# Row 1's bias and half of two rows' lo parts move between engines, and the first loads go through one queue

## The chip, the cores and the metric

The kernel runs on one core of one Trainium2 chip. A core has TensorE (matrix products; PE in the profile, PEld for its weight loads), VectorE (DVE), ScalarE (ACT), GpSimd (POOL) and SyncE (SP), which here only issues DMA transfers. SBUF is the on-chip memory with 128 partitions; PSUM holds the results of TensorE in eight banks of 128 x 512 float32. GpSimd reads and writes SBUF only in this kernel. The metric is device microseconds (us) from start to end of an execution, the median of some runs; lower is better.

## The reference

```python
# x: (4, 1024, 512), cond: (4, 256), W: (1536, 512), b: (512,)
hidden = concatenate([cond, cond], axis=-1)            # (4, 512)
x_mean = mean(x, axis=1, keepdims=True)                # (4, 1, 512)
fused = concatenate([x, x_mean * ones, hidden * ones], axis=-1)   # (4, 1024, 1536)
relation = relu(einsum('bld,do->blo', fused, W) + b)
out = x + relation
```

W falls into three parts of 512 rows. Only the first meets every row of x. The other two give one vector of 512 for each of the four batch rows r: mean(x) times the second part, plus cond times the sum of the two halves of the third part, plus b. That vector is the row's bias. So out = x + relu(x W_x + bias_r). All is float32.

## The kernel before, in words

**Tiles.** A row r has 8 tiles of 128 positions, so there are 32 tiles t = 0 to 31. A product needs x with its features on the partitions, so x must be turned. Four pieces j of 128 features each make up the sum, and each piece is multiplied in three matmuls, because a float32 value is split into hi (as rounded to the chip's fp32r type) and lo (the rest): hi by W's hi, hi by W's lo, lo by W's hi (L458 to L462). One tile takes 12 matmuls into one of five PSUM banks (pool ps_o).

**Turning.** Tiles are grouped in units: row 0 has units of 1, 1, 2 and 4 tiles, the other rows two units of 4. For row 0 TensorE turns the tiles of x against an identity matrix (L252). For rows 1 to 3 x is loaded a second time in 32-position blocks, as tile z, and VectorE turns those (L254). Either way the turned piece xT lies in PSUM, in a pool of two banks. ScalarE writes hi from it, and in the same instruction adds up the piece along the positions for the mean (L265); VectorE subtracts to get lo (L281). There are 15 buffers each of hi and lo. W's first part is split in the same way (w_hi on ScalarE, L233; w_lo on VectorE or GpSimd, L235).

**Bias.** VectorE adds up the sums of a row (total, L336) and forms acc = sum over j of total_j times W_mean_j plus the row's cond term (mean_term, L341, four instructions). The cond terms come from GpSimd and ScalarE (L332, L348, L353). acc is split into hi and lo (L357, L361), and two matmuls with a matrix of 1/1024 sum it over the partitions and spread it (bias_product, L373). What happens then depends on the row. Rows 0 and 1 (r < BY_PE = 2): the bias is split into a tile of 64 partitions, 32 with hi and 32 with lo (L384, L388), and a matmul with a 64 x 128 matrix "even" adds it into the tile's bank (L470); ScalarE applies relu straight from the bank (L480). Rows 2 and 3: ScalarE copies the bias to SBUF (L379), VectorE adds it to the bank's content into SBUF, which frees the bank (L477), and ScalarE applies relu there. The first three tiles (t < KEEP = 3) are finished before any bias is there: ScalarE copies their products to SBUF (L473), and VectorE adds the bias later (L477). GpSimd adds x (L485), SyncE stores (L497). There are ten output buffers. The last tile is done in two halves, with the bias product inside its bank, and VectorE does relu and the addition of x (L490).

**Order.** A planner in the file (class Plan) writes the order out beforehand. Each piece of work has a cost in us, an engine or two that may do it, what it depends on and an urgency; the planner keeps a clock for each engine, takes the work that could start first, and among work for that engine that could start within 0.1 us the most urgent. Every engine then works through its own instructions strictly in that order, as its inputs arrive. Loads and stores go through SyncE in such an order too.

**The first loads.** SyncE issues x of tile 0, of tile 1, of tiles 2 and 3, of tiles 4 to 7, then W's third part (w_cond) and W's second (w_mean), then the z loads of row 1 and on. Beside it ScalarE issues W's first part in four loads of 256 KB (L202). Eleven matmuls on zeros (L144) run ahead of all of it. The four loads of W have a buffer of their own; x tiles, in groups of four, share a pool of four buffers with w_cond.

The planner's line that makes a VectorE subtraction out of a piece, and the one that ties a turn to a free bank, are these:

```python
plan.add(("lo", c), {"dve": 0.15 + 0.135 * w}, [("hi", c)], urgent - 0.1, lambda e, c=c: split_lo(c))
if c >= 2:
    deps.append(("lo", c - 2))
```

Of the kernel before, what the change touches and what calls it, by code (L numbers as in the profile page):

```python
# [68 lines left out]
def kernel(  # L69
# [22 lines left out]
    nc = tc.nc  # L92
# [15 lines left out]
    Z_AHEAD, X_AHEAD, T_AHEAD = 24, 8, 7  # L108
    TURN_PE = (0, 1, 2, 3)
    BY_PE = 2  # L110
    KEEP = 3

# [53 lines left out]
    piece_of = {(u, j): c for c, (u, js) in enumerate(pieces) for j in js}  # L166
    first_piece = [min(c for (u, _), c in piece_of.items() if units[u][0] == r) for r in range(B)]
# [3 lines left out]
    w_x = const.tile([P, J, D], F32, name="w_x")  # L171
# [33 lines left out]
    plan.done["x", 1] = (9.8, 2.0, "sp")  # L205
# [4 lines left out]
    plan.done["cond"] = (12.7, 2.0, "sp")  # L210
    nc.sync.dma_start(out=w_mean, in_=Wv[1])
    plan.done["w_mean"] = (15.3, 2.0, "sp")
    plan.free["sp"] = 15.3
# [5 lines left out]
    x_order = [0, 1, None] + list(range(2, B * NK // G))  # L219
    for n, g in list(enumerate(x_order))[3:]:  # L220
        was = x_order[n - X_BUFS] if n >= X_BUFS else -1
        deps = ([] if was == -1 else [("add_cond", k) for k in range(KH)] if was is None else
                [("finished", was * G + i) for i in range(G)])
# [20 lines left out]
    def turn(c):  # L244
        u, js = pieces[c]
        n = units[u][2]
        v = xT[c] = ps_x.tile([P, G * P], F32, tag="x", name=f"xT{c}")
        if u in TURN_PE:
            for i in range(n):
                x_t = x_tile(last_tile[u] - n + 1 + i).rearrange("p (a j) -> p j a", j=J)  # L250
                for m, j in enumerate(js):
                    nc.tensor.transpose(v[:, (m * n + i) * P : (m * n + i + 1) * P], x_t[:, j], ident)  # L252
        else:
            nc.vector.transpose(  # L254
                v[:, : n * P].rearrange("p (n t) -> p n t", t=Q),
                zs[u].rearrange("p n (a j) -> p n j a", j=J)[:, : n * NQ, js[0], :],
            )

# [19 lines left out]
    def split_lo(c):  # L278
        u, js = pieces[c]
        m = units[u][2] * len(js) * P  # L280
        nc.vector.tensor_tensor(  # L281
            lo[c][:, :m], xT[c][:, :m], hi[c][:, :m].bitcast(F32), ALU.subtract
        )

    for c, (u, js) in enumerate(pieces):
        r, k0, n = units[u]

        urgent = 2 * c - 99.5 if not r else r * NK - T_AHEAD + (c - first_piece[r]) * 0.75
        deps = ([x_here(t) for t in range(last_tile[u] - n + 1, last_tile[u] + 1)]
                if u in TURN_PE else [("z", u, i) for i in range(NQ)])  # L290
        if c:
            deps.append(("turn", c - 1))
        if c >= 2:
            deps.append(("lo", c - 2))
            if len(pieces[c - 2][1]) > 1:
                deps.append(("sum", c - 2))
# [13 lines left out]
        if len(js) > 1:  # L310
            plan.add(("sum", c), {"dve": 0.65}, [("turn", c)], urgent + 0.1, lambda e, c=c: add_up(c))
# [52 lines left out]
    even32 = const.tile([2 * Q, P], F32, name="even32")  # L364
    nc.gpsimd.memset(even32, 1.0 / Q)
    even = const.tile([2 * Q, P], F32R, name="even")
    nc.gpsimd.tensor_copy(even, even32)

    def bias_product(r):
        m = 2 * Q if 0 < r < BY_PE else P  # L370
        pbs[r] = ps_b.tile([P, 512], F32, tag="b", name=f"pb{r}")
        for n, v in enumerate((acc_hi[r], acc_lo[r])):
            nc.tensor.matmul(  # L373
                pbs[r][:m], lhsT=mean[:, :m], rhs=v, start=(n == 0), stop=(n == 1)
            )
# [5 lines left out]
    def bias_hi(r):  # L381

        rows[r] = small.tile([2 * Q, D], F32R, tag="row", name=f"row{r}")
        nc.scalar.activation(rows[r], pbs[r][: 2 * Q], AF.Copy)  # L384

    def bias_lo(r):
        q = slice(Q, 2 * Q)
# [9 lines left out]
    for r in range(B):  # L397
        urgent = r * NK - 1.5 - 6 * (r == 0)
# [3 lines left out]
        for n in range(KH + J):  # L402
# [11 lines left out]
            else:  # L414
                deps = [("total", r), "w_mean"]
                if r and n == KH:
                    deps += [("bias", r - 1)] + [("bias_copy", 0)] * (r == 1)
# [8 lines left out]
        if r < BY_PE:  # L426
            plan.add(("bias_hi", r), {"act": 0.61}, [("bias_product", r)], urgent - 0.5,
                     lambda e, r=r: bias_hi(r))
            plan.add(("bias", r), {"dve": 0.69}, [("bias_hi", r)], urgent - 0.5,
                     lambda e, r=r: bias_lo(r))  # L430
            if not r:
                plan.add(("bias_copy", r), {"act": 0.61}, [("bias_product", r)], urgent - 0.4,
                         lambda e, r=r: bias_copy(r))
        else:
            plan.add(("bias", r), {"act": 0.61}, [("bias_product", r)], urgent - 0.5,
                     lambda e, r=r: bias_copy(r))
# [5 lines left out]
    def product(t, j, h=None):  # L442
# [15 lines left out]
        for n, (v, m) in enumerate(((hi, w_hi), (hi, w_lo), (lo, w_hi))):  # L458
            nc.tensor.matmul(  # L459
                pos[key][:, :w], lhsT=v[p][:, c], rhs=m[:, j, d],  # L460
                start=(h is None and j == 0 and n == 0), stop=((t < KEEP or r >= BY_PE) and j == J - 1 and n == 2),
            )  # L462
# [12 lines left out]
    def add_bias(t):  # L475
        o = o_tile(t)
        nc.vector.tensor_tensor(o, o if t < KEEP else pos[t], biases[t // NK], ALU.add)  # L477

# [20 lines left out]
    for t in range(NT):  # L499
        r, k = divmod(t, NK)  # L500
        u = unit_of[r, k]
        for h in (0, 1) if t == LAST else (None,):
            for j in range(J):
                c = piece_of[u, j]
                deps = [("hi", c), ("lo", c), ("w_hi", j), ("w_lo", j)]
                if j:
                    deps.append(("product", t, j - 1) if not h else ("product", (t, h), j - 1))
                elif h:
                    deps.append(("product", t, J - 1))
                else:  # L510
                    if t > 1:
                        deps.append(("product", t - 1, J - 1))
                    if t >= O_BANKS:
                        deps.append(("freed", t - O_BANKS))
                    if h == 0:
                        deps.append(("acc_lo", r))
                        deps.append(("freed", t + 1 - O_BANKS))
                plan.add(("product", (t, h) if h else t, j), {"pe": 0.7 if h is None else 0.36},
                         deps, t + 0.2 * j if t > 1 else 0.2 * j, lambda e, t=t, j=j, h=h: product(t, j, h))
        if t == LAST:  # L520
            for h in (0, 1):
                deps = [("product", (t, h) if h else t, J - 1), x_here(t)]
                if not h:
                    deps.append(("stored", t - O_BUFS))
# [4 lines left out]
        deps = [("product", t, J - 1), ("bias", r)]  # L529
        room = [("stored", t - O_BUFS)] if t >= O_BUFS else []  # L530
        if t < KEEP:
            plan.add(("freed", t), {"act": 0.6}, deps[:1], t, lambda e, t=t: keep(t))
            plan.add(("added", t), {"dve": 0.75}, [("freed", t), ("bias_copy", r)], t + 8, lambda e, t=t: add_bias(t))
            plan.add(("relu", t), {"act": 0.63}, [("added", t)], t + 8, lambda e, t=t: relu(t))
            biased = ("relu", t)
        elif r < BY_PE:
            plan.add(("biased", t), {"pe": 0.24}, deps, t, lambda e, t=t: bias_to_bank(t))
            plan.add(("freed", t), {"act": 0.63}, [("biased", t)] + room, t + 2, lambda e, t=t: relu(t))
            biased = ("freed", t)
        else:  # L540
            plan.add(("freed", t), {"dve": 0.7}, deps + room, t + 2, lambda e, t=t: add_bias(t))
# [3 lines left out]
            else:  # L545
                biased = ("freed", t)
# [37 lines left out]
```

## Time and profile before

| | us |
|---|---|
| median of 3 runs (117.93 to 118.69) | 118.6 |
| the profiled execution | 117.44 |
| its span, first to last instruction | 115.7 |
| TensorE busy | 107.7 |
| VectorE busy | 81.0 |
| GpSimd busy | 57.8 |
| ScalarE busy | 53.4 |

The profile comes from one execution. Its span is 1.7 us shorter than its time, since the time has a start and an end that the span leaves out. Busy times are sums over the whole span, and matmuls overlap one another, so that TensorE is called busy also where its matmuls follow slowly. The share of each stage has to be read from the stretches of the span. In a group of instructions, the number behind the x is how often it comes; behind the bar stand its busy time in all, the mean of one in ns, and the idle time of the engine ahead of it.

### The profile page before, as it was taken

The numbers are of one execution on the slowest core, as the hardware profiler recorded it, in microseconds if no ns is written. First come the engines' busy times: TensorE is split into PE (matmuls) and PEld (weight loads), VectorE is DVE, ScalarE is ACT, GpSimd is POOL, SyncE is SP. The second block draws the span as 40 slices with busy tenths as digits, with TensorE's granted clock in tenths as the row PEclk, the third lists the DMA queues.
The fourth block names the chain that finished last, engine by engine and source line by source line (L and its number), as shares of the span: only waits on it lengthen the run. The fifth ranks groups of instructions, "written<-read, shape, count | busy, mean of one in ns | idle before, by whom it ended". The sixth has DMA issues, their size and how long they took to land.

```text
span 115.7 us, 1477 instructions
## 1 busy us (share of the span) xinstructions
PE 107.7 (93%) x466; PEld 82.9 (72%) x466; DVE 81.0 (70%) x114; ACT 53.4 (46%) x122; POOL 57.8 (50%) x55
## 2 busy tenths in 40 slices
PE   5926999999999999999999999999999999999980
PEld 2415788888766687877766688887888878888870
DVE  1066734399999999976896999939999980632250
ACT  5055547887568460424963542246466140642200
POOL 6507144899809643040893029508354913199400
PEclk9998599999999999999999999999999999999999
DMA  3799999999999959999959999994422422025351
GB/s 109 179 392 396 394 370 198 203 203 205 205 256 281 199 136 207 304 388 390 349 177 213 272 397 407 400 258 176 164 91 106 169 91 91 0 91 222 140 227 45
DMA packets 22999, 26.31 MB, mean 227 GB/s; under 512 B 1228, under 2 KB 13776, under 8 KB 22864
## 3 DMA queue, kind: packets, MB, share of 16 engines
q1 hardware_dynamic: 22352, 25.17, 75.7%
q10 hardware_dynamic: 576, 1.05, 3.1%
q8 instruction: 3, 0.05, 0.2%
q14 instruction: 4, 0.03, 0.1%
q0 software_dynamic: 64, 0.01, 0.0%
HBM read 17.83 MB, written 8.39 MB: 227 GB/s over the span
## 4 chain that ended last, share of the span: by engine, by line
PE 89%; DMA 7%; SPq 1%; DVE 0%; issue 0%
PE po_None L459 77%; DMA x<-in_x_dram 7%; PE po_None L470 4%; PE xT L252 3%; PE po L459 2%; PE pb L373 2%; SPq L178 1%; PE po L455 0%; DVE o L490 0%; PE pt L324 0%
## 5 line engine op out<-in xcount | busy, mean ns | idle before, releaser
L485 POOL TENSOR_TENSOR o<-o,x 128x512 f32<-128x512 f32 x30 | 38.7, 1315 | 38.9 <-ACT o L480 32.1
L459 PE MATMUL po_None<-w_hi,hi 128*128 128x512 f32 x124 | 50.8, 409 | 0.0
L459 PE MATMUL po_None<-w_lo,hi 128*128 128x512 f32 x124 | 49.4, 398 | 0.0
L459 PE MATMUL po_None<-w_hi,lo 128*128 128x512 f32 x124 | 49.3, 398 | 0.0
L459 PEld LDWEIGHTS po_None<-w_hi,hi 128*128 128x128 f32 x124 | 23.5, 190 | 7.1 <-issue 1.6
L459 PEld LDWEIGHTS po_None<-w_hi,lo 128*128 128x128 f32 x124 | 23.6, 190 | 5.7
L459 PEld LDWEIGHTS po_None<-w_lo,hi 128*128 128x128 f32 x124 | 23.6, 190 | 5.0
L281 DVE TENSOR_TENSOR lo<-xT,hi 128x512 fp32r<-128x512 f32 (+1 forms) x34 | 21.9, 647 | 7.2 <-ACT hi L265 7.2
L254 DVE STREAM_TRANSPOSE xT<-z 128x512 f32<-128x512 f32 x24 | 26.2, 1102 | 0.3
L265 ACT ACTIVATE hi<-xT 128x512 fp32r<-128x512 f32 (+1 forms) x34 | 19.3, 571 | 9.3 <-DVE xT L254 5.5
L477 DVE TENSOR_TENSOR o<-po_None,bias 128x512 f32<-128x512 f32 x15 | 9.8, 677 | 12.2 <-ACT bias L379 4.1
L480 ACT ACTIVATE o<-o 128x512 f32<-128x512 f32 x17 | 10.5, 631 | 7.5 <-DVE o L477 7.5
L480 ACT ACTIVATE o<-po_None 128x512 f32<-128x512 f32 x13 | 7.5, 601 | 7.9 <-PE po_None L470 7.9
L341 DVE SCALAR_TENSOR_TENSOR acc<-w_mean,tot,acc 128x512 f32<-128x512 f32 x12 | 9.1, 756 | 0.4
L252 PE MATMUL xT<-ident,x 128*128 128x128 f32 x32 | 6.0, 307 | 3.5 <-DMA x<-in_x_dram 3.5
L252 PEld LDWEIGHTS xT<-ident,x 128*128 128x128 f32 x32 | 5.1, 207 | 4.6 <-issue 2.5
L357 ACT ACTIVATE acc_hi<-acc 128x512 fp32r<-128x512 f32 x4 | 2.4, 600 | 11.9 <-DVE acc L341 11.9
L265 ACT ACTIVATION_READ_ACCUMULATOR hi<-xT 128x1 f32 x32 | 6.4, 201 | 0.0
L353 POOL TENSOR_TENSOR cond<-bL,term 128x512 f32<-128x512 f32 x4 | 5.2, 1303 | 2.0 <-ACT term L348 2.0
L341 DVE SCALAR_TENSOR_TENSOR acc<-w_mean,tot,cond 128x512 f32<-128x512 f32 x4 | 5.7, 1426 | 0.6 <-POOL cond L353 0.3
L348 ACT ACTIVATE term<-wc,cT 128x512 f32<-128x512 f32 x8 | 5.6, 723 | 0.7 <-POOL cond L353 0.7
L353 POOL TENSOR_TENSOR cond<-cond,term 128x512 f32<-128x512 f32 x4 | 5.5, 1383 | 0.3
(54 smaller groups left out, 60.7 us busy)
## 6 DMA issues: line engine op xcount, KB each, us to landing
out_dram<-o SPq DMA_DIRECT2D x31, 256.0 KB, 2.4
x<-in_x_dram SPq DMA_DIRECT2D x7, 1024.0 KB, 7.9
z<-in_x_dram SPq DMA_DIRECT2D x24, 256.0 KB, 7.4
w_x<-in_L_cond_W_dram ACTq DMA_DIRECT2D x4, 256.0 KB, 7.2
w_cond<-in_L_cond_W_dram SPq DMA_DIRECT2D x1, 1024.0 KB, 12.7
w_mean<-in_L_cond_W_dram SPq DMA_DIRECT2D x1, 1024.0 KB, 12.6
x<-in_x_dram SPq DMA_DIRECT2D x2, 256.0 KB, 4.1
x<-in_x_dram SPq DMA_DIRECT2D x1, 512.0 KB, 8.0
```

The costliest lines, as they stand in the source:

```text
L252: nc.tensor.transpose(v[:, (m * n + i) * P : (m * n + i + 1) * P], x_t[:, j], ident)
L254: nc.vector.transpose(v[:, : n * P].rearrange("p (n t) -> p n t", t=Q), zs[u].rearrange("p n (a j) -> p n j a", j=J)[:, : n * NQ, js[0], :],)
L265: nc.scalar.activation(hi[c][:, :m], xT[c][:, :m], AF.Copy, accum_out=sums[:, r, js[0], s : s + 1] if len(js) == 1 else None,)
L281: nc.vector.tensor_tensor(lo[c][:, :m], xT[c][:, :m], hi[c][:, :m].bitcast(F32), ALU.subtract)
L341: nc.vector.scalar_tensor_tensor(acc[r], w_mean[:, j, :], totals[r][:, j : j + 1], acc[r] if j else conds[r], ALU.mult, ALU.add,)
L348: nc.scalar.activation(terms[r, k], wc[:, k], AF.Copy, scale=cT[:, k, r : r + 1])
L353: nc.gpsimd.tensor_tensor(conds[r], conds[r] if k else bL, terms[r, k], ALU.add)
L459: nc.tensor.matmul(pos[key][:, :w], lhsT=v[p][:, c], rhs=m[:, j, d], start=(h is None and j == 0 and n == 0), stop=((t < KEEP or r >= BY_P ...
L470: nc.tensor.matmul(pos[t], lhsT=even, rhs=rows[t // NK], start=False, stop=True)
L477: nc.vector.tensor_tensor(o, o if t < KEEP else pos[t], biases[t // NK], ALU.add)
L480: nc.scalar.activation(o_tile(t), pos[t] if KEEP <= t < BY_PE * NK else outs[t], AF.Relu)
L485: nc.gpsimd.tensor_tensor(outs[t], outs[t], x_tile(t), ALU.add)
```

## The change

- For rows 1 and 2, the pieces j = 1 and 3 of both units (8 of the 16) are turned by VectorE into SBUF, in a pool of two buffers, and their lo is made by GpSimd. The other pieces keep PSUM and VectorE. A turn waits for the lo of the piece two back of its own kind.
- BY_PE goes from 2 to 1: row 1's bias is copied to SBUF and added by VectorE, as in rows 2 and 3. Row 0 keeps the matmul, now with 128 rows (64 of hi, 64 of lo).
- The bias add of tiles 0 to 2 moves from VectorE to GpSimd.
- The first loads are all issued by SyncE in this order: x of tile 0, W's first 256 KB, x of tile 1, the other three of W, x of tiles 2 and 3, of 4 to 7, w_cond, w_mean.
- W's first part takes a buffer in the pool of x tiles; tiles 8 to 11 of x later get that buffer.
- Four more matmuls on zeros are put behind the turn of tile 0. Some urgencies change (T_AHEAD 7 to 8; the bias work of a row from 1.5 to 4 tiles ahead of it).

```diff
-    Z_AHEAD, X_AHEAD, T_AHEAD = 24, 8, 7
+    Z_AHEAD, X_AHEAD, T_AHEAD = 24, 8, 8
-    BY_PE = 2
+    BY_PE = 1
+    LO_POOL = {(r, u, j) for r in (1, 2) for u in (0, 1) for j in (1, 3)}
+    N_FILL = 4
+    by_pool = {c for c, (u, js) in enumerate(pieces)
+               if (units[u][0], units_of_row[units[u][0]].index(u), js[0]) in LO_POOL}
-    w_x = const.tile([P, J, D], F32, name="w_x")
+    w_x = xpool.tile([P, J, D], F32, tag="x", name="w_x")
-    for i, n in ((0, 1), (1, 1), (2, 2)):
-        load_x(0, i, n)
-        plan.done["x", 0, i] = (2.8 + 1.3 * i, 2.0, "sp")
-    for j in range(J):
-        nc.scalar.dma_start(out=w_x[:, j, :], in_=Wv[0, :, j])
-        plan.done["w", j] = (2.9 + 1.3 * j, 2.0, "sp")
-    load_x(1)
+    def load_w(j):
+        nc.sync.dma_start(out=w_x[:, j, :], in_=Wv[0, :, j])
+    for key, at, load in (
+        (("x", 0, 0), 2.7, lambda: load_x(0, 0, 1)),
+        (("w", 0), 4.3, lambda: load_w(0)),
+        (("x", 0, 1), 5.0, lambda: load_x(0, 1, 1)),
+        (("w", 1), 5.7, lambda: load_w(1)),
+        (("w", 2), 6.4, lambda: load_w(2)),
+        (("w", 3), 7.1, lambda: load_w(3)),
+        (("x", 0, 2), 8.4, lambda: load_x(0, 2, 2)),
+        (("x", 1), 11.0, lambda: load_x(1)),
+    ):
+        load()
+        plan.done[key] = (at, 2.0, "sp")
...
-        v = xT[c] = ps_x.tile([P, G * P], F32, tag="x", name=f"xT{c}")
+        if c in by_pool:
+            v = xT[c] = small.tile([P, G * P], F32, tag="xT", name=f"xT{c}")
+        else:
+            v = xT[c] = ps_x.tile([P, G * P], F32, tag="x", name=f"xT{c}")
...
+    def fill():
+        for _ in range(N_FILL):
+            nc.tensor.matmul(pw, lhsT=warm[:, :P], rhs=warm, start=True, stop=True)
+    plan.add(("fill",), {"pe": 0.22 * N_FILL}, [("turn", 0)], -99.4, lambda e: fill())
...
-        if c >= 2:
-            deps.append(("lo", c - 2))
+        same = [v for v in range(c) if (v in by_pool) == (c in by_pool)]
+        if len(same) >= 2:
+            deps.append(("lo", same[-2]))
-        plan.add(("lo", c), {"dve": 0.15 + 0.135 * w}, [("hi", c)], urgent - 0.1,
-                 lambda e, c=c: split_lo(c))
+        plan.add(("lo", c), {"pool": 1.33} if c in by_pool else {"dve": 0.15 + 0.135 * w},
+                 [("hi", c)], urgent - 0.1, lambda e, c=c: split_lo(e, c))
...
-    even = const.tile([2 * Q, P], F32R, name="even")
+    even = const.tile([P, P], F32R, name="even")
-        rows[r] = small.tile([2 * Q, D], F32R, tag="row", name=f"row{r}")
+        rows[r] = small.tile([P, D], F32R, tag="row", name=f"row{r}")
...
-        urgent = r * NK - 1.5 - 6 * (r == 0)
+        urgent = r * NK - 4 - 4 * (r == 0)
...
-            plan.add(("added", t), {"dve": 0.75}, [("freed", t), ("bias_copy", r)], t + 8, lambda e, t=t: add_bias(t))
+            plan.add(("added", t), {"pool": 1.33}, [("freed", t), ("bias_copy", r)], t + 8, lambda e, t=t: add_bias(e, t))
```

More of the change, by code (lines that the diff above doesn't have):

```diff
@@ L209 @@
     )
-    plan.done["cond"] = (12.7, 2.0, "sp")
+    plan.done["cond"] = (13.6, 2.0, "sp")
     nc.sync.dma_start(out=w_mean, in_=Wv[1])
-    plan.done["w_mean"] = (15.3, 2.0, "sp")
-    plan.free["sp"] = 15.3
+    plan.done["w_mean"] = (16.2, 2.0, "sp")
+    plan.free["sp"] = 16.2
     for n, u in enumerate(by_z):
@@ L218 @@
                      lambda e, u=u, i=i: load_z(u, i), later=3.0)
[L219 to L222, printed above, removed]
+    x_order = ["w", 0, 1, "cond"] + list(range(2, B * NK // G))
+    for n, g in list(enumerate(x_order))[4:]:
+        was = x_order[n - X_BUFS]
+        deps = ([("w_lo", j) for j in range(J)] if was == "w" else
+                [("add_cond", k) for k in range(KH)] if was == "cond" else
                 [("finished", was * G + i) for i in range(G)])
@@ L430 @@
                      lambda e, r=r: bias_lo(r))
[L431 to L435, printed above, removed]
+        if not r or r >= BY_PE:
+            plan.add(("bias_copy", r), {"act": 0.61}, [("bias_product", r)], urgent - 0.4,
                      lambda e, r=r: bias_copy(r))
@@ L460, in product @@
                 pos[key][:, :w], lhsT=v[p][:, c], rhs=m[:, j, d],
-                start=(h is None and j == 0 and n == 0), stop=((t < KEEP or r >= BY_PE) and j == J - 1 and n == 2),
+                start=(h is None and j == 0 and n == 0),
+                stop=(not KEEP <= t < BY_PE * NK and j == J - 1 and n == 2),
             )
@@ L502 @@
         for h in (0, 1) if t == LAST else (None,):
+            key = (t, h) if h else t
+            free = []
+            if t >= O_BANKS:
+                free.append(("freed", t - O_BANKS))
+            if h == 1:
+                free.append(("freed", t + 1 - O_BANKS))
+            if h == 0:
+                free.append(("acc_lo", r))
             for j in range(J):
@@ L536 @@
         elif r < BY_PE:
-            plan.add(("biased", t), {"pe": 0.24}, deps, t, lambda e, t=t: bias_to_bank(t))
+            plan.add(("biased", t), {"pe": 0.24}, whole + [("bias", r)], t, lambda e, t=t: bias_to_bank(t))
             plan.add(("freed", t), {"act": 0.63}, [("biased", t)] + room, t + 2, lambda e, t=t: relu(t))
@@ L540 @@
         else:
-            plan.add(("freed", t), {"dve": 0.7}, deps + room, t + 2, lambda e, t=t: add_bias(t))
+            plan.add(("freed", t), {"dve": 0.7}, whole + [("bias_copy", r)] + room, t + 2,
+                     lambda e, t=t: add_bias(e, t))
+            biased = ("freed", t)
             if t < NT - 2:
```

57 lines of the change are left out of this document (24 added, 33 removed).

## The prediction

> **What bounds the kernel now.** I read the page first, then the chain of waits in order of time, then the busy time by stretch of the opening, then the groups by line. The page gives the span and each engine's share.
>
> ```profile
> span 115.7 us, 1477 instructions
> PE 107.7 (93%) x466; PEld 82.9 (72%) x466; DVE 81.0 (70%) x114; ACT 53.4 (46%) x122; POOL 57.8 (50%) x55
> ```
>
> TensorE is busy nearly all the time. The chain (start, length, what) says whether that is the bound:
>
> ```profile
> 9.80 0.48 PE xT L252 x2
> 10.28 2.02 PE po_None L459 x6
> 12.30 0.43 PE xT L252 x2
> ...
> 13.03 0.63 PE xT L252 x2
> 13.66 1.71 PE po_None L459 x6
> ...
> 18.65 0.47 PE xT L252 x4
> ...
> 33.34 0.90 PE po_None L470 x3
> 34.23 1.60 PE po_None L459 x6
> 35.83 0.42 PE po_None L470
> 36.26 3.00 PE po_None L459 x12
> 39.26 0.43 PE po_None L470
> ...
> 54.35 1.35 PE po_None L470 x5
> 55.70 3.00 PE po_None L459 x12
> 58.70 0.43 PE po_None L470
> ...
> 76.44 21.69 PE po_None L459 x93
> ...
> 112.42 0.42 DVE o L490
> ```
>
> From 9.80 to 112.42 the chain never leaves TensorE: no product waits for data. So time is won only by fewer or quicker TensorE instructions, or by an earlier start, as long as the other engines keep up. Three things in it are not at the steady pace. A product matmul costs 21.69/93 = 0.233 us, but six take 2.02 and 1.71 near 10 to 15 us. A single bias matmul (L470) costs 0.42 to 0.43 itself, and the block behind it is 0.20 longer than its matmuls are worth (3.00 against 12 x 0.233 = 2.80; 1.60 against 1.40). And nothing is multiplied before 10.28.
>
> **The start.** Busy time by stretch (PE, PEld, DVE, ACT, POOL, then granted clock, DMA share, GB/s), and rows of the timeline and of the DMA issues (last number: us from issue to landing):
>
> ```profile
> 0.00:4.00 4.00, 2.81 (x7) 1.04 (x8) 0.35 (x3) 1.49 (x2) 2.87 (x11) 1.00 0.44 115
> 4.00:8.00 4.00, 2.32 (x13) 1.49 (x11) 1.37 (x3) 1.11 (x2) 0.52 (x3) 1.00 0.94 308
> 8.00:12.00 4.00, 2.20 (x8) 1.81 (x9) 2.86 (x6) 2.63 (x6) 2.53 (x2) 0.85 1.05 397
> 12.00:16.00 4.00, 4.00 (x20) 3.23 (x19) 1.83 (x5) 1.42 (x7) 0.02 (x1) 0.72 1.05 408
> ```
> ```profile
> 0.74 1.87 SPq L178 DMA_DIRECT2D x<-in_x_dram  x4
> 6.66 0.63 ACT L233 ACTIVATE w_hi<-w_x 128x512 fp32r<-128x512 f32 x1 [4.43 <-DMA w_x<-in_L_cond_W_dram]
> 6.84 0.34 SPq L211 DMA_DIRECT2D w_mean<-in_L_cond_W_dram  x1
> 7.33 0.69 DVE L235 TENSOR_TENSOR w_lo<-w_x,w_hi 128x512 fp32r<-128x512 f32 x1 [1.02 <-ACT w_hi L233]
> 9.80 0.48 PE L252 MATMUL xT<-ident,x 128*128 128x128 f32 x2 [2.18 <-DMA x<-in_x_dram]
> ```
> ```profile
> x<-in_x_dram SPq DMA_DIRECT2D x1, 256.0 KB, 2.5
> w_mean<-in_L_cond_W_dram SPq DMA_DIRECT2D x1, 1024.0 KB, 12.6
> ```
>
> Before: the first w_lo is there at 8.02, yet products start only after the turn at 9.80, which waits for tiles 2 and 3 (512 KB) in front of them in TensorE's order. Then the clock falls. The stretches show 0.85 and 0.72, and the chain's price is 0.48 + 2.02 + 0.43 + 0.63 + 1.71 = 5.27 us for 6 turns and 12 products that are worth 6 x 0.1175 (0.47/4) + 12 x 0.233 = 3.51: 1.76 lost. The start is as good as one at full clock at 9.80 + 1.76 = 11.56.
>
> After: the bytes moved, 0.46 MB at 4 us, 1.69 at 8, 3.28 at 12, are DMA's pace; the change deals them out in another order. In one queue W's first 256 KB ends at 0.52 MB (4.2 us), the fourth at 1.57 MB (7.6), tiles 2 and 3 at 2.10 (9.0), tiles 4 to 7 at 3.15 (11.7). Landing lags the bytes by 0.9 (the first x: 0.26 MB at 2.3 us, landed at 0.74 + 2.5 = 3.24) to 2.6 us (w_mean: 5.24 MB at 16.8, landed 6.84 + 12.6 = 19.44). I take 1.7: 5.9, 9.3, 10.7 and 13.4. So w_hi (0.63) and w_lo (0.69), with handovers, let tile 0 multiply from about 7.7. Tiles 0 and 1 hold 24 matmuls, 5.6 us, whose last quarter needs W's fourth piece at 9.3 + 0.63 + 0.69 = 10.6, in good time; I count a hole of 0.7 while tile 1 and the second piece of W arrive. That is a start worth 8.4, 3.15 us sooner. Bounds: 1.8 (W's first piece no sooner than 6.66, the larger lag) to 3.9 (no hole); 1.4 if the clock drops by the same 1.76 again. The four fill matmuls, 4 x 0.233 = 0.9 (1.7 at half clock), lie between the turn of tile 0, done near 5.6, and tile 1's landing near 7.3; without that cover they would cost their 0.9.
>
> The clock fell after TensorE stood idle for 1.3 and 2.2 us (6.87 and 9.80 are its only turns between 5.6 and 10). After the change no such gap stays beyond about 1 us, so I let it stay up. In the Trainium skill, TensorE: Matmul & The Clock Gate, Part 1, half rate comes only after a wholly idle window of about 3.4 us, and the windows run free. By that rule the clock should not have fallen here at all, and the trace differs (0.72); for the changed kernel the rule and my reading both keep 3.15, and only a repeat of the row would give 1.4.
>
> **The bias matmuls.** By the chain rows, row 1's eight (of the 13, row 0's five come first; then five together from 54.35 and three single) cost 1.35 + 0.20 + 3 x (0.43 + 0.20) = 3.44 us; they go entirely. Row 0's five stay, now with 128 rows instead of 64: 0.90 + 0.42 + 0.43 + 3 x 0.20 = 2.35 before. Where weights keep the full height there is no such gap:
>
> ```profile
> L470 PEld LDWEIGHTS po_None<-row,even 64*128 64x128 f32 x13 | 2.2, 184 | 2.8 <-issue 2.2 <-DVE lo L281 0.4
> L373 PEld LDWEIGHTS pb<-acc_lo,mean 128*128 128x128 f32 x3 | 0.6, 187 | 0.1
> ```
>
> The 64-row loads stood idle 2.8 us over 13, the 128-row ones of the mean product 0.1 over 3. So five at 0.233 = 1.17, a gain of 1.18 (bounds 0 and 1.18). Together TensorE saves 3.15 + 3.44 + 1.18 = 7.8 us, if it is fed.
>
> **What feeds it.** Groups by line, and the timeline around row 1's sum:
>
> ```profile
> L254 DVE STREAM_TRANSPOSE xT<-z 128x512 f32<-128x512 f32 x24 | 26.2, 1102 | 0.3
> L281 DVE TENSOR_TENSOR lo<-xT,hi 128x512 fp32r<-128x512 f32 x30 | 20.2, 677 | 5.3 <-ACT hi L265 5.2
> L341 DVE SCALAR_TENSOR_TENSOR acc<-w_mean,tot,acc 128x512 f32<-128x512 f32 x12 | 9.1, 756 | 0.4
> L235 POOL TENSOR_TENSOR w_lo<-w_x,w_hi 128x512 fp32r<-128x512 f32 x2 | 2.5, 1274 | 4.9 <-ACT w_hi L233 4.9
> L357 ACT ACTIVATE acc_hi<-acc 128x512 fp32r<-128x512 f32 x4 | 2.4, 600 | 11.9 <-DVE acc L341 11.9
> ```
> ```profile
> 42.97 0.14 DVE L336 TENSOR_REDUCE tot<-sums 128x4 f32<-128x16 f32 x1
> 43.18 1.29 POOL L485 TENSOR_TENSOR o<-o,x 128x512 f32<-128x512 f32 x1 [1.49 <-ACT o L480]
> 43.22 1.82 DVE L341 SCALAR_TENSOR_TENSOR acc<-w_mean,tot,cond 128x512 f32<-128x512 f32 x1
> 67.89 0.14 DVE L336 TENSOR_REDUCE tot<-sums 128x4 f32<-128x16 f32 x1
> ```
>
> An add or subtract of 128x512 on VectorE costs the 0.677 of lo. VectorE loses 8 lo (5.4), 3 adds for tiles 0 to 2 (2.0) and one bias_lo (0.7), and gains 8 bias adds of row 1 (5.4): 2.7 less. GpSimd gains 8 x 1.27 + 3 x 1.3 = 14, to 72 of a span near 108. A transpose into SBUF is in no row: I take the 1.10 of the one into PSUM, bounds 0.68 (the quickest 128x512 row) and 1.10 + 1.3 (it waits out one GpSimd instruction, below). ScalarE's work hardly moves.
>
> The new wait: with five banks, tile 13 needs tile 8's bank, and this is now freed by a VectorE add that needs row 1's bias. Before, row 1's sum stood at 42.97. After, four lo and one add are gone ahead of it: 42.97 - 4 x 0.68 - 0.67 = 39.6. From sum to freed bank: terms 1.82 + 3 x 0.756 = 4.1, acc_hi 0.6, acc_lo 0.68, mean product 0.47, copy 0.6, add 0.67, handovers 0.5: 7.6, so 47.2. TensorE ended tile 12 at 54.35; less 3.15 and 1.18 that is 50.0. Slack 2.8. Row 2: sum to sum took 67.89 - 42.97 = 24.9; less four lo, two adds and bias_lo (4.7), plus eight adds (5.4), 25.6, so 65.2 at worst and about 62 if the idle time inside (VectorE's 81.0 of 115.7) shrinks; plus 7.6 that is 69.6 to 72.8, against 50.0 + 8 x 2.80 + 0.47 = 72.9. Slack 0 to 3. Row 3 is worked as before. So supply keeps up, barely; I take 0.5 us of stalls. If this fails, behind the waiting product stand all later products, and behind the waiting add VectorE's turns of the next row. The two lo that tile 8 needs from GpSimd take 1.27 where VectorE took 0.68, 0.6 more each, inside the same slack as long as GpSimd does its other adds behind them.
>
> **The sum.** 7.8 - 0.5 = 7.3 off the profiled execution's 117.44 gives 110.1. That execution lies 1.2 below the median of 118.6; in the median's terms 111.3.
>
> **The rivals.** *VectorE's chain comes no sooner* (its lo removed only leave more waiting). Row 1's bias was usable on TensorE at 54.35; a bank freed then stalls tile 13 by 54.35 - 50.0 = 4.3, and row 2 perhaps another 0.7. Gain 2.8: 115.8. For it: slack of 0 to 3 us, an order that is fixed ahead. Against: four lo do go. *The start gains only its lower end or the clock falls again*: 7.3 - 1.8 = 5.5, 113.1. *Slower: the transposes into SBUF and GpSimd lock each other out.* The rows show such a lock: the first term (w_mean and cond in SBUF) took 1.82 instead of 0.756 and began as GpSimd did (43.18), ending 0.57 after it. If each of the eight transposes waits out 1.3 us, VectorE is 5.2 late per row, 10.4 by row 2's bias; less a slack of 0 to 3 that stalls TensorE 7.4 to 10.4, and lo on GpSimd is held as well. Gain 7.8 - 10.4 = 2.6 us lost: 121. It decides from about 1 us of wait each. Against: the transposes before ran beside GpSimd at 1.10 throughout (one SBUF operand, though PSUM was the other).
> The Trainium skill, SBUF — State Buffer, Who interferes with whom, says that VectorE contends with GpSimd when it has two SBUF inputs or runs in a two-port mode with SBUF at both ends; the trace agrees on the first (1.82), and no run shows whether this transpose enters the second.
> *It does not do what it says*: the order is written by a planner from costs of its own, and a bad one could cost the whole gain, near 118.6.
>
> **How the numbers follow.** The forecast, 109.7 to 112.6: 0.5. Weak start or clock: 0.12. VectorE's chain: 0.22. No net change: 0.08. The lock: 0.08. The range needs the first three, with the last one cut at 116.3, and begins at 109.7. One per cent is 1.2 us, about what a measurement here can tell: faster 0.84, same 0.08, slower 0.08.
>
> **What would show it.** First product near 7.7 and a granted clock near 1 from 8 to 16. No L470 after row 0, and its five at 0.23 without longer blocks behind. Transposes at 1.1 into SBUF. In the chain, no wait at tile 13, 21 or 29: an add of bias just ahead of a product there proves the first rival; transposes of 2 us beside GpSimd prove the lock.

## The result, and the profile after

The changed kernel took 111.24 us (median of 4 runs, 110.68 to 111.58), the kernel before beside it 118.27 (4 runs, 116.19 to 118.69). The ratio is 0.950, with an interval of 0.935 to 0.964; a ratio leaves out executions more than 1.5% above the fastest of their kernel, here two of the kernel before. The forecast was 111.3. The profiled execution took 110.68 us against 117.44 before, so 6.76 us are to be found in the traces, where the prediction's sum had 7.3. The page has the span and the engines' shares:

```profile
span 108.9 us, 1482 instructions
PE 103.3 (95%) x462; PEld 81.6 (75%) x462; DVE 76.1 (70%) x112; ACT 54.0 (50%) x122; POOL 69.9 (64%) x64
```

VectorE has 4.9 us less work (2.7 was forecast) and GpSimd 12.1 more (14 was forecast). The chain of waits (start, length, what) again never leaves TensorE once products run without a gap, from 9.83 on:

```profile
9.83 1.44 PE po_None L478 x5
11.27 0.47 PE xT L268 x4
...
13.37 0.68 PE xT L268 x4
...
29.25 0.45 PE pb L395 x2
...
31.79 0.84 PE po_None L490 x3
32.63 0.70 PE po_None L478 x3
33.33 0.23 PE po_None L490
33.56 2.79 PE po_None L478 x12
36.35 0.23 PE po_None L490
...
47.52 18.19 PE po_None L478 x78
65.70 0.47 PE pb L395 x2
66.17 23.09 PE po_None L478 x99
...
105.66 0.42 DVE o L511
```

The last addition starts at 105.66, before it was 112.42: 6.76 less. Three parts of it can be read off.

- **Row 1's bias matmuls** are gone, and from 47.52 on nothing stands between the products but the mean product (pb): 3.44 us, by the prediction's rows.
- **Row 0's five** cost 0.84 + 0.23 + 0.23 = 1.30, and the block of 12 behind a single one takes 2.79, as any 12 products do (12 x 0.233). Before they cost 2.35: 1.05 won.
- **The start.** Row 0's mean product (pb) is the first mark that both chains have. Before, it came at 30.08 with 66 of the chain's products done. Now it comes at 29.25, with 68 from 9.83 on and 4 ahead of that. At before's pace 6 products more would have brought 30.08 + 6 x 0.233 = 31.48. So the start won 2.23 us.

That is 6.72 of the 6.76. Nothing is left for a stall of products in rows 1 to 3.

The busy time by stretch (PE, PEld, DVE, ACT, POOL, then granted clock, DMA share, GB/s) shows the clock kept up, and how full the engines are around row 1's bias:

```profile
8.00:12.00 4.00, 3.13 (x14) 2.39 (x15) 3.67 (x6) 2.36 (x7) 0.00 (x0) 1.00 1.05 396
12.00:16.00 4.00, 4.00 (x23) 3.21 (x23) 2.08 (x6) 1.72 (x9) 0.10 (x1) 1.00 1.07 410
...
30.00:54.00 24.00, 24.00 (x104) 19.20 (x103) 22.46 (x28) 15.75 (x39) 23.78 (x20) 1.00 1.17 241
```

Before, the clock was 0.85 and 0.72 in the first two of these. In the last, which holds row 1's bias, GpSimd is busy 23.78 us of 24 and VectorE 22.46: TensorE is fed, with little to spare. The timeline (start, length, engine, line, what; in brackets the idle time before and its releaser) shows where the start was slower than forecast, and how row 1's bias met tile 13:

```profile
6.69 0.69 DVE L296 TENSOR_REDUCE sums<-xT 128x4 f32<-128x512 f32 x1 [5.47 <-ACT hi L287]
7.23 0.49 PE L478 MATMUL po_None<-w_hi,hi 128*128 128x512 f32 x1
7.30 0.68 DVE L303 TENSOR_TENSOR lo<-xT,hi 128x512 fp32r<-128x512 f32 x1
7.89 0.68 DVE L248 TENSOR_TENSOR w_lo<-w_x,w_hi 128x512 fp32r<-128x512 f32 x1
8.63 0.50 PE L478 MATMUL po_None<-w_lo,hi 128*128 128x512 f32 x1 [0.91 <-DVE w_lo L248]
9.83 0.50 PE L478 MATMUL po_None<-w_lo,hi 128*128 128x512 f32 x1 [0.24 <-DVE w_lo L248]
...
48.19 0.69 DVE L496 TENSOR_TENSOR o<-po_None,bias 128x512 f32<-128x512 f32 x1 [0.48 <-ACT bias L401]
...
50.84 0.40 PE L478 MATMUL po_None<-w_hi,hi 128*128 128x512 f32 x1
```

The first product runs at 7.23, but the next needs w_lo, and VectorE makes in one row the sum of tile 0, its lo and w_lo, then the next sum and the next w_lo. TensorE waits until 8.63 and again until 9.83. The add that frees tile 8's bank ends at 48.19 + 0.69 = 48.88, and tile 13 (its first product is the last line) starts at 50.84 without a wait. Groups by line (count, then busy us, mean ns, idle before):

```profile
L270 DVE STREAM_TRANSPOSE xT<-z 128x512 f32<-128x512 f32 x24 | 25.7, 1090 | 0.0
L490 PEld LDWEIGHTS po_None<-row,even 128*128 128x128 f32 x5 | 0.9, 188 | 0.5 <-POOL cond L376 0.3
```

All 24 transposes, the eight into SBUF among them, take 1.09 us on average; before, into PSUM, they took 1.10. The loads of the 128-row weights take 0.188, as the products' loads do.

### The profile page after: what moved, and what is told of

It reads as the page before. It is cut to its first block, busy times and chain, and to the rows that moved or that the text cites. A ratio compares the mean times of both kernels' runs of the same rounds, so it can differ in the third digit from the quotient of the medians.

```text
span 108.9 us, 1482 instructions
## 1 busy us (share of the span) xinstructions
PE 103.3 (95%) x462; PEld 81.6 (75%) x462; DVE 76.1 (70%) x112; ACT 54.0 (50%) x122; POOL 69.9 (64%) x64
## 4 chain that ended last, share of the span: by engine, by line
PE 92%; DVE 3%; issue 1%; ACT 1%
PE po_None L478 79%; PE pw L147 4%; PE xT L268 3%; PE po L478 3%; PE pb L395 2%; PE po_None L490 1%; DVE w_lo L248 1%; DVE sums L296 1%; ACT hi L287 1%; PE po L474 0%; DVE o L511 0%; DVE lo L303 0%; DVE warm L138 0%; PE pt L347 0%; DVE ones L140 0%
## 5 line engine op out<-in xcount | busy, mean ns | idle before, releaser
L506 POOL TENSOR_TENSOR o<-o,x 128x512 f32<-128x512 f32 x30 | 39.5, 1328 | 18.5 <-ACT o L501 15.4
L478 PE MATMUL po_None<-w_hi,hi 128*128 128x512 f32 x124 | 49.4, 399 | 0.0
L270 DVE STREAM_TRANSPOSE xT<-z 128x512 f32<-128x512 f32 x24 | 25.7, 1090 | 0.0
L496 DVE TENSOR_TENSOR o<-po_None,bias 128x512 f32<-128x512 f32 x23 | 15.4, 678 | 13.7 <-POOL o L506 5.9
L303 DVE TENSOR_TENSOR lo<-xT,hi 128x512 fp32r<-128x512 f32 (+1 forms) x26 | 16.4, 640 | 6.2 <-ACT hi L287 6.1
L501 ACT ACTIVATE o<-o 128x512 f32<-128x512 f32 x25 | 15.5, 630 | 9.4 <-DVE o L496 9.4
L303 POOL TENSOR_TENSOR lo<-xT,hi 128x512 fp32r<-128x512 f32 x8 | 10.9, 1369 | 0.0
L355 POOL TENSOR_TENSOR wc<-w_cond 128x512 f32<-128x512 f32 x2 | 2.6, 1302 | 11.3 <-DMA w_cond<-in_L_cond_W_dram 11.3
L401 ACT ACTIVATE bias<-pb 128x512 f32<-128x512 f32 x4 | 2.4, 597 | 9.0 <-PE pb L395 9.0
L147 PE MATMUL pw<-warm 128*128 128x512 bf16 x11 | 4.4, 577 | 1.2 <-DVE ones L140 1.2
```

Of the source, the lines that this page charges most:

```text
L147: nc.tensor.matmul(pw, lhsT=warm[:, :P], rhs=warm, start=True, stop=True)
L270: nc.vector.transpose(v[:, : n * P].rearrange("p (n t) -> p n t", t=Q), zs[u].rearrange("p n (a j) -> p n j a", j=J)[:, : n * NQ, js[0], :],)
L303: nc_of[e].tensor_tensor(lo[c][:, :m], xT[c][:, :m], hi[c][:, :m].bitcast(F32), ALU.subtract)
L478: nc.tensor.matmul(pos[key][:, :w], lhsT=v[p][:, c], rhs=m[:, j, d], start=(h is None and j == 0 and n == 0), stop=(not KEEP <= t < BY_PE ...
L496: nc_of[e].tensor_tensor(o_tile(t), outs[t] if t < KEEP else pos[t], biases[t // NK], ALU.add)
L501: nc.scalar.activation(o_tile(t), pos[t] if KEEP <= t < BY_PE * NK else outs[t], AF.Relu)
```

## The experiments

Each ratio is against the kernel before, run beside it on the same chip (its medians 117.58 to 117.69 us). The changed kernel's own is 0.950 [0.935, 0.964]. Ends of chains compare with 112.42 before and 105.66 after.

### The start

**The load order alone**, in the kernel before, with W in a buffer of its own and no fill (shortened; the done-times given to the planner are those of the changed kernel):

```diff
-    for i, n in ((0, 1), (1, 1), (2, 2)): load_x(0, i, n)
-    for j in range(J): nc.scalar.dma_start(out=w_x[:, j, :], in_=Wv[0, :, j])
-    load_x(1)
+    load_x(0, 0, 1); load_w(0); load_x(0, 1, 1); load_w(1); load_w(2); load_w(3)
+    load_x(0, 2, 2); load_x(1)      # load_w(j): the same DMA, by nc.sync
```

> The kernel before with the new order of the first loads on one queue alone, W still in its own buffer, no fill. My theory: products start near 7.5 to 8.6 and tiles 0 and 1 are multiplied before tiles 2 and 3 land, so 2.6 us less than before if the granted clock stays up from 10 to 14 us (about 115.7 where before has 118.3), 0.8 less if it falls as before (117.5). Rival (two queues land their loads sooner than one): start later than 9.8, time at or above before.

114.54 us (114.41 to 114.59), ratio 0.980 [0.971, 0.988]. Its chain, and one stretch:

```profile
9.47 1.43 PE po_None L466 x5
...
28.87 0.45 PE pb L380 x2
```
```profile
12.00:16.00 4.00, 4.00 (x25) 3.31 (x24) 1.75 (x6) 1.74 (x7) 0.41 (x1) 1.00 1.06 409
```

Row 0's mean product comes with the same 72 products done as after: 31.48 - 28.87 = 2.61 us won at the start (its turn of tile 0 began at 5.19, 0.36 sooner than after). The clock stays at 1.00 without the fill, over the whole span in all four executions. So the new order by itself does what the start did, clock included.

**The fill taken out** of the changed kernel:

```diff
-    plan.add(("fill",), {"pe": 0.22 * N_FILL}, [("turn", 0)], -99.4, lambda e: fill())
```

> The changed kernel without the four fill matmuls behind the turn of tile 0. If they keep the clock up: granted clock below 0.9 in some stretch between 7 and 15 us and up to 1.8 us more, 113.0. If the earlier products alone keep it up: 111.2, or up to 0.2 less, since the turn of tile 1 does not stand behind them. I hold the first for the likelier, 6 to 4, since TensorE would stand idle for about a microsecond three times between 6 and 10 us.

110.6 us (110.25 to 110.91), ratio 0.942 [0.937, 0.946], clock 1.00 from 4 to 16 us. The four matmuls buy nothing here; that they cost something is not shown either, since the interval overlaps the changed kernel's.

**The loads put back** in the changed kernel as they were before, with the planner's done-times for them, the fill kept (shortened):

```diff
-    (the loads of the changed kernel, all by nc.sync)
+    for i, n in ((0, 1), (1, 1), (2, 2)): load_x(0, i, n)
+    for j in range(J): nc.scalar.dma_start(out=w_x[:, j, :], in_=Wv[0, :, j])
+    load_x(1)
```

> The changed kernel with the first loads as before: x on SyncE's queue, W's four pieces on ScalarE's; the four fill matmuls and all else stay. My theory (the order of the loads sets when products start): they start again behind the turn of tiles 2 and 3, near 9.8 us, and the start that is worth 9.0 in the changed kernel becomes 9.8 with the clock kept by the fill (+0.8 us, 112.0) or 11.6 with the clock down (+2.6, 113.8). Rival (the start moved because of the fill and the other edits, not because of the order): no change, 111.2, and a first product before 9 us.

The four executions took 119.32, 120.38, 111.44 and 114.93 us: too far apart for a ratio. The profiled one is that of 119.32, and the loads are not what it lost most by. Its timeline, the group of the mean product, and two stretches:

```profile
38.48 2.53 POOL L499 TENSOR_TENSOR o<-o,x 128x512 f32<-128x512 f32 x2
39.71 8.13 DVE L357 SCALAR_TENSOR_TENSOR acc<-w_mean,tot,cond 128x512 f32<-128x512 f32 x1
...
46.00 1.28 POOL L489 TENSOR_TENSOR o<-o,bias 128x512 f32<-128x512 f32 x1
```
```profile
L388 PE MATMUL pb<-acc_hi,mean 128*128 128x512 f32 x4 | 2.0, 495 | 4.8 <-DVE acc_lo L377 4.8
```
```profile
48.00:52.00 4.00, 0.00 (x0) 0.00 (x0) 3.93 (x6) 0.77 (x2) 0.00 (x0) 0.83 0.54 199
52.00:56.00 4.00, 3.58 (x8) 2.81 (x9) 4.00 (x6) 2.87 (x9) 3.09 (x3) 0.50 0.10 27
```

The first term of row 1's sum, which takes 0.756 us where nothing holds it, was on VectorE for 8.13. Through all that time GpSimd ran seven instructions without a gap, from 38.48 to 47.28; the term ended 0.56 after the last. Row 1's acc_lo came that much later, and TensorE, at the mean product in its fixed order, waited 4.8 us for it. The granted clock was 1.00 until 50.5, long after the term began, and fell to 0.50 during this wait: the lower clock followed the stall. So this run alone does not tell what the loads are worth, and it asks a question of its own: is it the term's two SBUF operands (w_mean and cond)?

**The same with one SBUF operand.** ScalarE first copies cond into acc's PSUM bank, and the first term adds to acc like the others:

```diff
+    def cond_copy(r):
+        acc[r] = ps_b.tile([P, D], F32, tag="b", name=f"acc{r}")
+        nc.scalar.activation(acc[r], conds[r], AF.Copy)
-            acc[r], w_mean[:, j, :], totals[r][:, j : j + 1], acc[r] if j else conds[r],
+            acc[r], w_mean[:, j, :], totals[r][:, j : j + 1], acc[r],
```

> The changed kernel with the first loads as before (the earlier run of that, 111.4 to 120.4 us), and with one edit more: ScalarE first copies a row's cond term into the PSUM bank of acc, so that VectorE's first term instruction reads one SBUF operand instead of two. In the earlier run's trace that instruction took 8.13 us at row 1 and ended 0.56 us after a train of GpSimd adds without a gap. My theory (VectorE's two-SBUF instruction waits for GpSimd and can be passed over again and again while GpSimd's adds follow without a gap): all first terms 0.76 us, no stall of TensorE before tile 13, and times within 2 us of each other, 111.5 to 114 by how late W's pieces land. Rival (the 8 us came from elsewhere): the first terms still reach several us in some execution, and times go up to 120 again.

111.63 us (111.47 to 113.42), ratio 0.952 [0.944, 0.960]. All 16 terms now take the same time, and the chain ends at 106.62:

```profile
L355 DVE SCALAR_TENSOR_TENSOR acc<-w_mean,tot,acc 128x512 f32<-128x512 f32 x16 | 12.1, 756 | 1.9 <-ACT acc L362 1.3
```

GpSimd had no gap here either: it was busy 4.00 of the 4 us from 40 to 44, in which row 1's four terms ran. So the stall of the profiled execution was the term's second SBUF operand beside GpSimd. The Trainium skill, SBUF — State Buffer, Who interferes with whom, says that VectorE with two SBUF inputs contends with a GpSimd instruction that reads SBUF; the trace agrees (8.13 against 0.756). Whether the other two executions above 112 us had the same stall was not traced. And with the clock up in this run (1.00 from 4 to 16), the old order of loads costs 106.62 - 105.66 = 0.96 us by the ends of the chains, and 1.07 by row 0's mean product (29.62 with 69 products done, so 30.32 with 72, against 29.25).

**The sums later.** Without the fill, and with the sums of tiles 0 and 1 behind their lo and w_lo on VectorE; and the same with the copy of cond:

```diff
-            plan.add(("sum", c), {"dve": 0.65}, [("turn", c)], urgent + 0.1, lambda e, c=c: add_up(c))
+            plan.add(("sum", c), {"dve": 0.65}, [("lo", c), ("w_lo", c)], urgent + 0.1, lambda e, c=c: add_up(c))
```

> The changed kernel without the fill, and with VectorE's sums over tiles 0 and 1 put behind those tiles' lo and the w_lo of the same number. In the changed kernel sum, lo and w_lo of tile 0 follow one another from 6.69 to 8.57, and the second matmul of tile 0 waits for that w_lo until 8.63. My theory (the start now hangs on VectorE's order, not on the loads): w_lo of the first piece ends 0.6 us sooner, the second one 0.4, products without a gap from about 9.3 instead of 9.83: 0.4 to 0.6 less, 110.0 to 110.6. Rival (W's pieces land too late for that): the same as without the fill, 110.6.

> The run before, plus the copy of the cond term into PSUM by ScalarE. If a wait of VectorE for GpSimd costs nothing here, because row 1's bias has 2.1 us to spare: the same time as the run before, within 0.3 us, with first terms of 0.76 us where the changed kernel has up to 1.47. If it costs: up to 0.7 less. The copy adds 0.6 us on ScalarE to the chain of each row's bias where the cond term comes last, as in row 0; no effect expected.

The first took 110.59 us (110.22 to 110.89), ratio 0.944 [0.937, 0.951]; the second 110.32 (109.88 to 110.79), 0.942 [0.934, 0.949]. The steady products of the second begin here, and its chain ends at 104.86:

```profile
9.22 1.43 PE po_None L482 x5
```

From the end of the first hi to the steady products it is 2.57 us in both (7.21 to 9.78, and 6.65 to 9.22), against 3.16 in the changed kernel (6.67 to 9.83): the 0.6 of one sum. In the first it does not show in the end, since the turn of tile 0 began at 6.06 there instead of 5.55. That beginning moved between 5.19 and 6.07 us from run to run, as the eleven matmuls on zeros ahead of it end sooner or later. The second is the lowest median of all, but its interval overlaps the changed kernel's, so that it is faster is not shown.

### The bias matmuls

**128 rows of weights alone**, in the kernel before, rows 0 and 1:

```diff
-    even32 = const.tile([2 * Q, P], F32, name="even32")
-    nc.gpsimd.memset(even32, 1.0 / Q)
-    even = const.tile([2 * Q, P], F32R, name="even")
+    even32 = const.tile([P, P], F32, name="even32")
+    nc.gpsimd.memset(even32, 2.0 / P)
+    even = const.tile([P, P], F32R, name="even")
-        m = 2 * Q if 0 < r < BY_PE else P
-        rows[r] = small.tile([2 * Q, D], F32R, tag="row", name=f"row{r}")
+        rows[r] = small.tile([P, D], F32R, tag="row", name=f"row{r}")
-        q = slice(Q, 2 * Q)
+        q = slice(P // 2, P)
```

> The kernel before with row 0's and row 1's bias matmuls on 128 rows of weights instead of 64, nothing else. My theory (a weight load of another height than the one before stops the overlap of load and matmul): the 13 bias matmuls cost 13 x 0.233 = 3.0 us instead of 5.8 in the chain, 2.8 us less than before (about 115.5). Rival (the gap is the wait of the bias matmul for its inputs): the single ones keep 0.42 and a block 0.20 longer behind them, time as before.

114.7 us (113.5 to 115.72), ratio 0.977 [0.964, 0.991]. From its chain, a load near the start, and row 1:

```profile
2.11 8.35 DMA w_x<-in_L_cond_W_dram
...
51.95 1.16 PE po_None L469 x5
53.12 2.82 PE po_None L458 x12
55.94 0.23 PE po_None L469
56.18 2.80 PE po_None L458 x12
```

A single bias matmul costs 0.23, and the block behind it takes 2.80 to 2.82 where it took 3.00. All thirteen cost 0.69 + 0.23 + 0.23 in row 0 and 1.16 + 3 x 0.23 in row 1, 3.00 us, where they cost 2.35 + 3.44 = 5.79. In this execution the clock also stayed up with the old loads, and its end, 108.45, is 3.97 sooner than before: 2.79 by the weights, and 1.18 by the start, where the chain now goes through the load of the first line (2.11 + 8.35 = 10.46). In the other three executions of this kernel the mean clock was 0.970 to 0.982; the median, 2.9 below the kernel before's, fits the weights alone.

**64 rows again**, in the changed kernel (row 0 only; the diff above the other way round):

> The changed kernel with row 0's five bias matmuls on 64 rows again. My theory: the five cost 2.35 us instead of 1.30 in the chain, 1.05 more than the changed kernel (112.3). Rival (their inputs now come in time, so height does not matter): 111.2.

111.93 us (111.62 to 112.16), ratio 0.957 [0.950, 0.964].

```profile
31.62 0.90 PE po_None L490 x3
32.52 0.90 PE po_None L478 x3
33.41 0.43 PE po_None L490
33.84 2.99 PE po_None L478 x12
```

The 0.43 and the 0.20 behind each are back: 0.90 + 2 x 0.43 + 3 x 0.20 = 2.36 against 1.30. The chain ends 0.91 later, with the products 0.23 sooner at the start (9.60). By the rows it is the change of height that costs, and not the 64 rows as such: before, the three together took 0.90 = 0.43 + 2 x 0.235 and the five 1.35 = 0.43 + 4 x 0.23, so that only the first of them is dear, and the block behind the last.

**Row 1's bias on TensorE again**, in the changed kernel, with 128 rows:

```diff
-    BY_PE = 1
+    BY_PE = 2
```

> The changed kernel with row 1's bias as a matmul on TensorE again, with 128 rows of weights. My theory (what counts is TensorE's time): eight more matmuls of 0.233 us, 1.9 more: 113.1. If the height of the weights were not the reason for the dear bias matmuls, eight of them cost 3.4 as before: 114.6. Rival (VectorE binds at tile 13, and the add of bias there costs as much as it saves): 111.2.

113.0 us (112.2 to 113.61), ratio 0.963 [0.954, 0.971].

```profile
49.78 0.93 PE po_None L490 x4
50.72 1.40 PE po_None L478 x6
52.12 0.23 PE po_None L490
```

Eight cost 0.93 + 4 x 0.23 = 1.85, as 8 x 0.233 do, and the chain ends 1.95 later (107.61), 0.20 of it by a later start (10.03 against 9.83). So of row 1's 3.44 us, 1.6 were to be had by 128 rows alone, and the move to VectorE brought the other 1.85.

**Row 0's bias on VectorE too**:

```diff
-    BY_PE = 1
+    BY_PE = 0
```

> The changed kernel with row 0's bias, too, added by VectorE (no bias matmul at all). TensorE saves 5 x 0.233 = 1.2 us. If VectorE's chain to row 1's bias has but 2.1 us to spare at tile 13, then five adds more and one bias_lo less, 4 x 0.68 = 2.7 us, and TensorE 1.2 us earlier make a stall of about 1.8 there: 111 to 112, no gain. If VectorE has more to spare than I read: 110.0.

111.38 us (110.51, 111.2, 111.55 and one of 117.78 that was not traced and stays open), ratio 0.950 [0.939, 0.962]. The 1.17 us of matmuls are gone, and a wait has their place, in tile 8 and not, as I had expected, in tile 13:

```profile
35.38 0.61 DVE o L496
35.99 0.14 issue
36.12 8.65 PE po_None L478 x36
```

Ahead of these lines the chain runs through VectorE's turns and lo of row 1 from 31.12, and there through a load of z.

### lo on GpSimd

**All lo on VectorE, all turns into PSUM**:

```diff
-    LO_POOL = {(r, u, j) for r in (1, 2) for u in (0, 1) for j in (1, 3)}
+    LO_POOL = set()
```

> The changed kernel with all lo of rows 1 and 2 on VectorE and all turned pieces in PSUM, as before. My theory (VectorE's chain to row 1's bias has 2.1 us to spare at tile 13: the add that frees tile 8's bank ends at 48.9, tile 13 starts at 51.0): four lo more ahead of the sum, 4 x 0.68 = 2.7 later, so a stall of 0.6 us or, with two banks only for turned pieces, up to 2, before tile 13: 111.8 to 113.2. Rival (VectorE has slack enough, lo on GpSimd buys nothing): 111.2 and no wait in the chain.

112.35 us (111.56 to 113.43), ratio 0.954 [0.948, 0.961]. TensorE's timeline:

```profile
53.68 0.40 PE L478 MATMUL po_None<-w_hi,lo 128*128 128x512 f32 x1
54.97 0.50 PE L478 MATMUL po_None<-w_hi,hi 128*128 128x512 f32 x1 [0.89 <-DVE o L496]
```

Tile 14 should follow at 53.68 + 0.233 = 53.91 and starts at 54.97, after tile 9's add: a stall of 1.06. VectorE had no gap from 49.86 up to that add. With a start that was 0.46 later (10.29) this explains its end, 107.12, which is 1.46 us behind the changed kernel's.

**The eight pieces in SBUF, but their lo on VectorE**:

```diff
-        plan.add(("lo", c), {"pool": 1.33} if c in by_pool else {"dve": 0.15 + 0.135 * w},
+        plan.add(("lo", c), {"dve": 0.15 + 0.135 * w},
```

> The changed kernel with the eight pieces still turned into SBUF, but their lo made by VectorE, which then reads two SBUF operands while GpSimd works. If VectorE and GpSimd shut each other out for such an instruction (the first acc term took 1.82 us instead of 0.76 in the kernel before): a mean of these lo between 1.0 and 1.9 us instead of 0.68, a bias of row 1 that comes 3 to 6 us later, and 112 to 115 us. Without a lock: 0.68 each, and the time of the run with all lo on VectorE.

112.23 us (111.71 to 112.9), ratio 0.956 [0.949, 0.962]. TensorE's and VectorE's timeline, and VectorE's group:

```profile
38.42 1.67 DVE L303 TENSOR_TENSOR lo<-xT,hi 128x512 fp32r<-128x512 f32 x1
...
53.84 0.40 PE L478 MATMUL po_None<-w_hi,lo 128*128 128x512 f32 x1
55.45 0.50 PE L478 MATMUL po_None<-w_hi,hi 128*128 128x512 f32 x1 [1.22 <-DVE o L496]
```
```profile
L303 DVE TENSOR_TENSOR lo<-xT,hi 128x512 fp32r<-128x512 f32 x30 | 22.8, 770 | 4.1 <-ACT hi L287 4.0
```

The stall is 55.45 - 54.07 = 1.38. The eight lo with both operands in SBUF cost 22.8 - 22 x 0.677 = 7.9 us, 0.99 each, up to 1.75, if the others cost the 0.677 that they cost before. So taking lo off VectorE saves a stall of 1.1 to 1.4 us: less than the 5.4 us of work that it takes off, since VectorE had some slack and only what delays row 1's bias and the adds right behind it showed.

## Why the prediction was right

**The size.** 111.3 was forecast and 111.24 measured; in the traces 7.3 us and 6.76. The start was off one way and the stalls the other, so that the sum came out closer than its parts: that is luck. So is the agreement of the medians to 0.06: the profiled execution lies 0.56 below its median here, where the forecast took over the 1.2 of the kernel before.

**The start: 3.15 forecast, 2.23 measured; this term was mis-sized.** The step that failed is "I count a hole of 0.7". The first product came at 7.23, even before the 7.7. But between it and 11.11, where the next turn begins, nine products took 3.88 us instead of 2.10: a hole of 1.78. I had put it down to loads still to arrive; the trace names VectorE's sum, lo and w_lo, and putting the sum later took 0.6 of it away. The 1.1 of hole too much and the 0.47 gained on the first product explain 0.6 of the 0.92. Of the other 0.3, 0.2 is the turn at 13.37, which took 0.68 us where the one at 11.27 took 0.47. It stands right behind the two small matmuls of cond (pt); whether these cause it was not tested. In the kernel before I had put such a turn (0.63 us for two, at 13.03) wholly down to the clock. The parts of this term are now known too. With the old loads a clock that stays up is worth about 1.2, not the 1.76 that I took from the slow rows. The run of 128 rows won 1.18 at the start; there the products next wait for a piece of W that lands at 10.46, and the third turn began 0.70 sooner than before (9.10 against 9.80), so that the split is rough. The executions of the kernel before agree: the two with a mean granted clock of 0.998 took 116.24 and 116.25 us, eleven of the thirteen at 0.983 to 0.985 took 117.07 to 117.79. The order of loads is worth about 1.0 beside that (0.96 by putting it back).

**The clock stayed up**, as forecast. The fill has no part in it: without it, the clock stayed up as well.

**The bias matmuls: 3.44 + 1.18 forecast, 3.44 + 1.05 measured.** The reading that the lower height of the weights costs 0.2 before and behind was right, and the runs show it from both sides: 2.79 won in the kernel before, 1.06 lost in the changed one, and row 1's eight at 1.85 with 128 rows. The five cost 1.30 and not 1.17, since the first three took 0.84 together, behind a short wait; the profile names cond (0.3), and VectorE's half of the row, which they also need, was ready only at 31.55.

**The supply: 0.5 us of stalls forecast, none measured.** The slack at tile 13 was to be 2.8 and is 50.84 - 48.88 = 1.96: the add ended at 48.88, 1.7 later than worked out, with TensorE 0.8 later too. Row 1's sum stood at 39.50, as forecast (39.6); the 1.7 came behind it, where acc_lo stood after a lo and a turn in VectorE's order (45.06), and the mean product at 46.90 in TensorE's. That it was a matter of 2 us was right: with lo on VectorE, in either form, TensorE stalls by 1.06 and 1.38.

**The rivals.** *VectorE's chain comes no sooner* fell for the changed kernel. In a milder form it is what happens without GpSimd's share: row 1's sum then stands at 41.81, against 42.97 before and 39.50 after, and TensorE stalls by 1.06 where the rival had 4.3. *A weak start* fell: 2.23 lies above its 1.8. *The lock* fell for the transposes (1.057 to 1.128 us, bounds 0.68 to 2.4). It is real for the instruction from which I argued: at 8.13 us in one execution it held far longer than the 1.3 that I gave a wait, and the changed kernel still has that place. Its own first terms took 0.98 on average, the longest 1.47. *That the order gets no better* fell.

## What to carry to other kernels

When one engine is on the chain from end to end, look in its chain for pieces that cost more than their count times the steady pace: here one matmul with weights of another height cost 0.63 us instead of 0.23, and weights filled up to the full height cost nothing more. Moving work off an engine that is not the bottleneck pays only as far as a wait ends sooner by it: 5.4 us off VectorE were worth 1.1 to 1.4. And a second SBUF operand that costs little most of the time stalled a whole row in one traced execution, beside a GpSimd without a gap. A copy of one operand into PSUM took that away; where GpSimd is filled to 23.78 us of 24 it is worth trying.

## What the runs showed of the hardware

- A VectorE instruction with two SBUF operands was held through seven GpSimd instructions in a row, 8.13 us, not through one. At the same place in the changed kernel, with GpSimd about as full, it took 1.47, and the longest in the other traces was 2.94 (row 2, in the run without bias matmuls). What decides how long it is held stays open.
- Weights of another height than those of the load before cost TensorE 0.20 us at the change and 0.20 at the change back (0.43 for a single matmul, 0.20 more in the block behind it), and nothing between them.
- The clock fell in the kernel before about 1 us after waits of 1.3 and 2.2 us, and stood at 0.50 from 10.8 to 14.2 us (read from stretches of 0.25 us). In the first run with the loads put back it fell at 50.6, within a wait that began when the last product ended at 47.65, and stood at 0.50 until 57.4. The Trainium skill, TensorE: Matmul & The Clock Gate, Part 1, asks for a wholly idle window of about 3.4 us; with 3.0 us idle the second case comes near it, and the first does not fit. Waits of 0.91 (changed kernel) and 1.65 (the run of 128 rows) left the clock at 1.00.
